# Layer 1 of a four-layer kernel: score products read from PSUM on VectorE, sums over heads by identity products on TensorE, expert shares applied to an input

## The chip, the cores and the metric

The kernel runs on one core of one Trainium2 chip. A core has a matrix engine (TensorE, PE; its weight loads are listed as PEld), a vector engine (VectorE, DVE), an activation engine (ScalarE, ACT), a general engine (GpSimd, POOL) and queues for transfers. They run side by side and wait for each other by semaphores; each works through its own queue in order. SBUF is the working memory, PSUM the memory that TensorE writes its products to. The metric is the time of one execution in microseconds (us), the median of several runs. A profile is one execution recorded by the hardware; L12 is line 12 of the kernel before.

## The reference

Four layers, each `x = x + s * g` with `s` an attention-like branch and `g` the silu of a feed-forward branch, both on the layer norm of x. There are 4 sequences of 1024 tokens with 128 features. The change touches only the second layer (called layer 1). Its attention works inside a token, between its 16 heads of 8 features:

```
x = (y_de * mask).reshape(c, t, HEADS, PER_DIM)
q = x @ Wq.T + bq;  k_ = x @ Wk.T + bk;  v = x @ Wv.T + bv
scores = einsum('cthd,ctgd->cthg', q, k_) * scale
attn = entmax15(scores, axis=-1)
out = einsum('cthg,ctgd->cthd', attn, v)
```

The sum over d has 8 terms, the sum over g has 16, and both are different for every token. `entmax15` sorts the 16 scores of a head, takes running sums of the sorted values and of their squares, finds a threshold from them, and squares what lies above it. The feed-forward branch takes two of eight experts for each token:

```
expert_out = einsum('etf,efh->eth', silu(x w1) * (x w3), w2)
out = einsum('te,eth->th', combine, expert_out)
```

`combine` holds a token's weight for each expert, zero for all but two. The kernel computes all eight experts for all tokens and lets `combine` choose.

## The kernel before

Everything is kept in fp32. Layer 1 runs over eight units; a unit is 512 tokens, as four tiles of 128 tokens, tokens on the partitions. For each unit there are two generators, `heads1` for attention and `moe1` for the experts. Each gives work out in steps that end at a `yield`.

`heads1`: for each of the four tiles TensorE multiplies the transposed input with a block-diagonal weight matrix, 384 columns of queries, keys and values (L701); VectorE adds the bias on the way from PSUM to SBUF (L702); POOL multiplies each head's query with each head's key, 2048 products per token (L707); VectorE sums over d with a reduction (L710). Then VectorE sorts the 16 scores of every row in ten min and max steps (`sort16`, L683 and L684; ACT copies the parts that a step leaves alone, L673 and L674). The threshold follows on VectorE, POOL and ACT in turns: z, the distance from the top score (L720, POOL), two running sums (L724 and L725, VectorE), their division by the rank (L730 and L731, POOL), the clamp at zero (L734, VectorE), a square root (L735, ACT), tau (L738, POOL), a comparison with z and a count (L740 and L742, VectorE), the choice of one tau (L743, VectorE, and L744, POOL), and the share of each head (L748, POOL, and L751, VectorE). Last come the values: for each tile POOL multiplies shares and values, 2048 products per token (L756), and VectorE sums over g (L759).

`moe1`: logits (L767), the two best experts (`top2`, L189 to L197), their weights (L773 to L780). Then for each expert two halves of 128 hidden features: two products with 512 token columns (L786 and L788), the silu on ACT (L789), a multiplication on VectorE (L790). The down product puts tokens on the partitions, eight products of 128 columns (L795), and VectorE scales them by the expert's weight and adds them up, four instructions for an expert (L799 and L801). A silu on ACT makes g (L802).

`update` multiplies s by g and adds the result to x, both on POOL (L225 and L226).

`weave` decides the order in which these pieces are written down: it always takes the generator that is least far along, counting each generator's steps against a given number of steps. A unit's attention after its scores, its experts, and the next unit's scores (`upto`) are woven together. The framework then puts the instructions into the engines' queues, by its own scheduling, and the order in a queue can differ from the order in which they were written. Once built, it is fixed. Tiles come from pools: a tag has a number of buffers, and an instruction that writes a new tile waits until the last reader of the buffer's former tile is done. The PSUM pools of layer 1 are "mm" with four buffers, "tr" with two and "o" with two. `transpose_tiles` (L122) transposes by TensorE, and its copies from PSUM go to VectorE (L112) or ACT (L114).

Of the kernel before, what the change touches and what calls it, by code (L numbers as in the profile page):

```python
# [18 lines left out]
P = 128  # L19
# [72 lines left out]
class Kit:  # L92
# [86 lines left out]
    def top2(self, pool, score, n_tiles, tag):  # L179

        nc = self.nc
        shape4 = [P, n_tiles, 8, 8]
        cmp = pool.tile(shape4, F32, tag=tag + "_cmp", name="cmp")
        eq = pool.tile(shape4, F32, tag=tag + "_eq", name="eq")
        rank = pool.tile([P, n_tiles, 8], F32, tag=tag + "_rank", name="rank")
        before = self.c("before").rearrange("p (e j) -> p e j", j=8)
        other = score.unsqueeze(2).to_broadcast(shape4)
        own = score.unsqueeze(3).to_broadcast(shape4)
        nc.vector.tensor_tensor(cmp, other, own, ALU.is_gt)  # L189
        nc.vector.tensor_tensor(eq, other, own, ALU.is_equal)  # L190
        flat = lambda a: a.rearrange("p t e j -> p t (e j)")
        wide = self.c("before").unsqueeze(1).to_broadcast([P, n_tiles, 64])
        nc.gpsimd.tensor_tensor(flat(eq), flat(eq), wide, ALU.mult)
        nc.gpsimd.tensor_tensor(flat(cmp), flat(cmp), flat(eq), ALU.add)
        nc.vector.tensor_reduce(rank, cmp, AX.X, ALU.add)
        two = pool.tile([P, n_tiles, 8], F32, tag=tag + "_two", name="two")
        nc.vector.tensor_scalar(two, rank, 2.0, None, op0=ALU.is_lt)  # L197
        return two
# [417 lines left out]
def layer1(k, W, x_all, eps5, ps):  # L616

    nc, tc = k.nc, k.tc
    with tc.tile_pool(name="l1", bufs=1) as p1, tc.tile_pool(name="l1d", bufs=2) as p2:
# [6 lines left out]
        def start(half, b):  # L626
# [13 lines left out]
            s, g = (p2.tile([P, HT, D], F32, tag=tag, name=tag) for tag in ("s", "g"))  # L640
            return x, s, g, heads1(k, W, p1, p2, ps, xnT, maskedT, s, keep), moe1(k, W, p1, p2, ps, xnT, g)
# [8 lines left out]
        for n in range(len(units)):  # L650
            x, s, g, heads, moe = now
            parts = [(heads, 19), (moe, 18)]
            if n + 1 < len(units):
                now = start(*units[n + 1])
                parts.append((upto(now[3]), 4))
            weave(*parts)
            k.update(x, s, g)
# [34 lines left out]
def heads1(k, W, p1, p2, ps, xnT, maskedT, s, keep):  # L692
# [3 lines left out]
    qkv = p2.tile([P, 4, 3, P], F32, tag="qkv", name="qkv")  # L696
    score = p2.tile([P, 4, 16, 16], F32, tag="score", name="score")
    for t in range(4):
        lhsT = maskedT if maskedT is not None and t == 0 else xnT[:, t * P : (t + 1) * P]
        pq = ps.tile([P, 512], F32, tag="mm", name="pq")  # L700
        nc.tensor.matmul(pq[:, 0:384], lhsT, W["bd"].rearrange("p n c -> p (n c)"), start=True, stop=True)  # L701
        nc.vector.tensor_tensor(  # L702
            qkv[:, t].rearrange("p n c -> p (n c)"), pq[:, 0:384], W["bias"].rearrange("p n h d -> p (n h d)"), ALU.add
        )
        heads = lambda n: qkv[:, t, n, :].rearrange("p (h d) -> p h d", d=8)
        prod = p2.tile([P, 16, 16, 8], F32, tag="prod", name="prod")
        nc.gpsimd.tensor_tensor(  # L707
            prod, heads(0).unsqueeze(2).to_broadcast([P, 16, 16, 8]), heads(1).unsqueeze(1).to_broadcast([P, 16, 16, 8]), ALU.mult
        )
        nc.vector.tensor_reduce(score[:, t], prod, AX.X, ALU.add)  # L710
        yield "scores" if t == 3 else None
# [4 lines left out]
    new = lambda name: p2.tile([P, R * 16], F32, tag=name, name=name)  # L716
# [34 lines left out]
    nc.vector.scalar_tensor_tensor(attn, t1, 0.0, t1, op0=ALU.max, op1=ALU.mult)  # L751
    for t in range(4):
        a = attn.rearrange("p (t h g) -> p t h g", t=4, g=16)[:, t]
        v = qkv[:, t, 2, :].rearrange("p (g d) -> p d g", d=8)
        prod = p2.tile([P, 16, 8, 16], F32, tag="prod", name="prod")
        nc.gpsimd.tensor_tensor(  # L756
            prod, a.unsqueeze(2).to_broadcast([P, 16, 8, 16]), v.unsqueeze(1).to_broadcast([P, 16, 8, 16]), ALU.mult
        )
        nc.vector.tensor_reduce(s[:, t, :].rearrange("p (h d) -> p h d", d=8), prod, AX.X, ALU.add)  # L759
        yield  # L760


def moe1(k, W, p1, p2, ps, xnT, g):
# [5 lines left out]
    nc.vector.tensor_copy(logit.rearrange("p t e -> p (t e)"), pl[:, 0:32])  # L769
    two = k.top2(p2, logit, HT, "m1")  # L770
# [9 lines left out]
    nc.vector.tensor_tensor(comb, comb, best.unsqueeze(2).to_broadcast([P, HT, 8]), ALU.mult)  # L780
    for e in range(8):
        yield
        h = p2.tile([P, 2, 512], F32, tag="h", name="h")
        for c in range(2):
# [3 lines left out]
            nc.tensor.matmul(pu, W["w3"][:, e, c * P : (c + 1) * P], xnT, start=True, stop=True)  # L788
            nc.scalar.activation(h[:, c, :], pg, AF.Silu)  # L789
            nc.vector.tensor_tensor(h[:, c, :], h[:, c, :], pu, ALU.mult)  # L790
        yield
        po = ps.tile([P, 4, D], F32, tag="o", name="po")
        for t in range(4):
            for c in range(2):
                nc.tensor.matmul(po[:, t, :], h[:, c, t * P : (t + 1) * P], W["w2"][:, e, c, :], start=(c == 0), stop=(c == 1))  # L795
        for t in range(4):
            w = comb[:, t, e : e + 1]
            if e == 0:
                nc.vector.tensor_scalar(g[:, t, :], po[:, t, :], w, None, op0=ALU.mult)  # L799
            else:  # L800
                nc.vector.scalar_tensor_tensor(g[:, t, :], po[:, t, :], w, g[:, t, :], op0=ALU.mult, op1=ALU.add)  # L801
    nc.scalar.activation(g, g, AF.Silu)  # L802
# [1131 lines left out]
def tile_kernel(ctx: ExitStack, tc: tile.TileContext, I, out):  # L1934
# [30 lines left out]
    with tc.tile_pool(name="w2", bufs=1) as w2:  # L1965
        with tc.tile_pool(name="raw2", bufs=1) as raw2:
            W2 = load2(k, w2, raw2, I)
            with ExitStack() as st:
                ps = PsumTags(st, tc, {"mm": 4, "tr": 2, "o": 2}, "ps1")
# [36 lines left out]
```

## Time and profile before

Three runs took 3631.48, 3636.46 and 3638.12 us; the median is 3636.46. The profiled execution took 3631.55 us, its span is 3629.8 us.

| what | value |
|---|---|
| profiled execution; its span | 3631.55; 3629.8 us |
| busy over the span: PE, VectorE, ACT, POOL | 64%, 69%, 41%, 37% |
| layer 1, from the first query product to the last addition to x | 579.6 to 1391.4 us |
| busy in 578 to 1395 us: PE, VectorE, ACT, POOL | 457.7, 640.2, 212.3, 469.8 us |
| granted TensorE clock there | 0.77 of full speed |
| transfers there | 3 GB/s |

In the lists of groups a row gives line, engine, operation, output<-inputs, shapes, number of instructions, then busy time and mean length, then the idle time of the engine just before these instructions and what ended it. An fp32 product is listed as two TensorE instructions. [...] In timelines the columns are the start, the time covered, engine, line, operation, tiles and the number of instructions put together in the row.

### The profile page before, as it was taken

The numbers are of one execution on the slowest core, as the hardware profiler recorded it, in microseconds if no ns is written. First come the engines' busy times: TensorE is split into PE (matmuls) and PEld (weight loads), VectorE is DVE, ScalarE is ACT, GpSimd is POOL, SyncE is SP. The second block draws the span as 40 slices with busy tenths as digits, with TensorE's granted clock in tenths as the row PEclk, the third lists the DMA queues.
The fourth block names the chain that finished last, engine by engine and source line by source line (L and its number), as shares of the span: only waits on it lengthen the run. The fifth ranks groups of instructions, "written<-read, shape, count | busy, mean of one in ns | idle before, by whom it ended". The sixth has DMA issues, their size and how long they took to land. (4 is left out here: it accounts for less than half of the span.)

```text
span 3629.8 us, 51798 instructions
## 1 busy us (share of the span) xinstructions
PE 2314.1 (64%) x18736; PEld 1376.0 (38%) x18737; DVE 2504.9 (69%) x5864; ACT 1470.2 (41%) x3148; POOL 1347.2 (37%) x1089
## 2 busy tenths in 40 slices
PE   4877875555655564966643400058888889889885
PEld 2555553333333332642100100035555555545553
DVE  5555557778888775556778677744787677677767
ACT  4555543222222224244432300015665655565553
POOL 3344444665555653225365222243122122212222
PEclk9888987778877786966555555566776766767666
DMA  3000001000000001211334399727466466566553
GB/s 82 1 1 1 1 1 31 0 0 1 0 1 0 0 0 44 96 58 34 69 52 73 63 111 102 117 70 211 127 196 199 139 191 200 156 181 199 170 167 108
DMA packets 486565, 295.16 MB, mean 81 GB/s; under 512 B 165392, under 2 KB 473484, under 8 KB 485284
## 3 DMA queue, kind: packets, MB, share of 16 engines
q1 hardware_dynamic: 485156, 287.65, 32.9%
q10 hardware_dynamic: 1152, 4.19, 0.4%
q8 instruction: 147, 2.41, 0.3%
q14 instruction: 110, 0.90, 0.1%
HBM read 156.43 MB, written 134.74 MB: 80 GB/s over the span
## 5 line engine op out<-in xcount | busy, mean ns | idle before, releaser
L1808 POOL TENSOR_SCALAR_AFFINE_SELECT rel<-rel 128x512 f32<-128x512 f32 x288 | 179.9, 635 | 765.3 <-DMA rel<-flat 493.1
L1863 ACT ACTIVATE neg<-neg,low 128x640 f32<-128x640 f32 (+7 forms) x512 | 390.5, 766 | 165.5 <-DVE low L1856 164.8
L1649 DVE STREAM_TRANSPOSE wT<-neg 128x640 f32<-128x640 f32 (+7 forms) x512 | 364.3, 756 | 54.0 <-ACT neg L1863 29.6
L1841 PE MATMUL score<-k,q 8*128 8x512 f32 (+3 forms) x1536 | 331.2, 742 | 90.0 <-DVE low L1856 89.6
L1856 DVE CUSTOM_DVE_ANT_0 neg<-score,rel,low 128x128 f32<-128x128 f32 (+3 forms) x448 | 218.1, 519 | 149.7 <-PE score L1841 71.7
L795 PE MATMUL po<-w,h 128*128 128x128 f32 x1024 | 172.3, 329 | 170.6 <-DVE h L790 170.5
L1777 PE MATMUL pr<-emb,q 8*128 8x256 f32 x1024 | 257.7, 566 | 30.4 <-ACT r L1779 22.8
L1877 PEld LDWEIGHTS po<-wT,vb 128*32 128x32 f32 x10240 | 200.2, 136 | 150.4 <-issue 101.2
L1877 PE MATMUL po<-wT,vb 128*32 128x64 f32 (+1 forms) x10240 | 234.6, 253 | 31.3 <-issue 17.5
L795 PEld LDWEIGHTS po<-w,h 128*128 128x128 f32 x1024 | 161.4, 238 | 235.9 <-DVE h L790 208.1
L1779 ACT COPY r<-pr 128x512 f32<-128x512 f32 x256 | 138.9, 582 | 160.7 <-PE pr L1777 77.0
L1777 PEld LDWEIGHTS pr<-emb,q 8*128 8x128 f32 x1024 | 152.9, 265 | 127.7 <-ACT r L1779 61.6
L1841 PEld LDWEIGHTS score<-k,q 8*128 8x128 f32 x1536 | 123.4, 251 | 165.6 <-DVE low L1856 103.2
L707 POOL TENSOR_TENSOR prod<-qkv 128x2048 f32<-128x2048 f32 x32 | 153.2, 4789 | 75.7 <-DVE qkv L702 74.2
L786 PE MATMUL pg<-xnT,w 128*128 128x512 f32 x256 | 145.2, 651 | 56.1 <-DVE qkv L702 53.5
L756 POOL TENSOR_TENSOR prod<-rest,qkv 128x2048 f32<-128x2048 f32 x32 | 171.6, 5385 | 12.0 <-DVE rest L751 10.7
L1856 DVE CUSTOM_DVE_ANT_0 neg<-score,rel 128x512 f32<-128x512 f32 (+3 forms) x320 | 149.6, 521 | 34.8 <-PE score L1841 30.9
L122 PE MATMUL pt<-const_sb,o 128*128 128x128 f32 x8 | 3.0, 432 | 266.1 <-DVE o L1376 266.1
L788 PE MATMUL pu<-xnT,w 128*128 128x512 f32 x256 | 138.7, 625 | 11.0 <-ACT h L789 5.7
L789 ACT ACTIVATE h<-pg 128x512 f32<-128x512 f32 x128 | 75.5, 596 | 167.7 <-PE pg L786 167.2
L987 ACT ACTIVATE h<-ph 128x512 bf16<-128x512 f32 (+1 forms) x128 | 72.0, 590 | 173.7 <-PE ph L986 171.3
L986 PE MATMUL ph<-xin,upT 128*128 128x512 bf16 (+1 forms) x128 | 74.0, 612 | 103.1 <-DVE xin L980 103.1
(613 smaller groups left out, 5875.9 us busy)
## 6 DMA issues: line engine op xcount, KB each, us to landing
flat<-r SPq DMA_DIRECT2D x256, 256.0 KB, 2.8
rel<-flat SPq DMA_DIRECT2D x112, 512.0 KB, 3.9
flat<-r SPq DMA_DIRECT2D x256, 128.0 KB, 2.9
rel<-flat SPq DMA_DIRECT2D x96, 256.0 KB, 4.2
kt<-kd SPq DMA_DIRECT2D x64, 128.0 KB, 7.2
qt<-qd SPq DMA_DIRECT2D x64, 128.0 KB, 6.7
ktc<-ktd SPq DMA_DIRECT2D x32, 256.0 KB, 5.7
kdc<-kdd SPq DMA_DIRECT2D x32, 256.0 KB, 6.0
```

The costliest lines, as they stand in the source:

```text
L707: nc.gpsimd.tensor_tensor(prod, heads(0).unsqueeze(2).to_broadcast([P, 16, 16, 8]), heads(1).unsqueeze(1).to_broadcast([P, 16, 16, 8]), AL ...
L756: nc.gpsimd.tensor_tensor(prod, a.unsqueeze(2).to_broadcast([P, 16, 8, 16]), v.unsqueeze(1).to_broadcast([P, 16, 8, 16]), ALU.mult)
L786: nc.tensor.matmul(pg, W["w1"][:, e, c * P : (c + 1) * P], xnT, start=True, stop=True)
L795: nc.tensor.matmul(po[:, t, :], h[:, c, t * P : (t + 1) * P], W["w2"][:, e, c, :], start=(c == 0), stop=(c == 1))
L1649: nc.vector.transpose(weights[at, pair][j][:, t % 2, 0 : (t + 1) * P], S[j][:, 0 : (t + 1) * P])
L1777: nc.tensor.matmul(to[:, m, :], q[at, t * P : (t + 1) * P], W["emb"][at, i, :], start=True, stop=True)
L1779: nc.scalar.copy(r[:, n], to)
L1808: nc.gpsimd.affine_select(out=rel[:, :, slot(back), :], in_=rel[:, :, slot(0), :], compare_op=op, fill=fill, base=0, pattern=[[0, 4], [-si ...
L1841: nc.tensor.matmul(sc[:, j, 0 : last - first], q[at(j), 1 + t * P : 1 + n], kk[at(j), first:last], start=True, stop=True)
L1856: nc.vector.tensor_tensor_reduce(out=neg[:, begin:last], in0=sc[:, j, begin - first : last - first], in1=rel[:, j, slot : slot + (last - b ...
L1863: nc.scalar.activation(neg[:, 0:n], neg[:, 0:n], AF.Exp, bias=here, scale=-1.0, accum_out=group["sums"][:, j, t : t + 1])
L1877: nc.tensor.matmul(o[32 * j : 32 * j + 32, 2 * pair + m.start : 2 * pair + 2, :], vb[:, kb, j].rearrange("p a d -> p (a d)"), weights[j][: ...
```

## The change

Attention. The bias is now added by TensorE itself, as a second product of a row of ones with one row of the bias into the same PSUM tile. ACT copies keys and values to SBUF; the queries stay in PSUM. VectorE, not POOL, multiplies queries, read in PSUM, with keys, read in SBUF, and writes the products with d outermost. TensorE sums over d: eight products of the identity matrix with 256 columns each, added up in one PSUM tile, which ACT copies to the scores. The products of a tile are summed one step later than they are made. The share of each head is made by two ACT instructions, Relu and Square, in place of one on VectorE. POOL still multiplies shares and values, now with g outermost, and TensorE sums over g with sixteen identity products of 128 columns for each tile; ACT copies the four sums to s.

Experts. The weights of a unit are split into three bf16 parts (`thirds`), transposed, and for each expert spread over all partitions by a product with a constant (`shares`). VectorE multiplies the transposed input with that share, and this weighted input goes into the linear branch (w3), so that the weight is already in the hidden features. The down product now has w2 as its stationary side and 512 token columns, and adds up all eight experts in one PSUM tile. The result is transposed (gT), so `update` turns it back by TensorE, multiplies s by it on VectorE and adds to x on POOL. `top2` reads one of its two inputs in PSUM.

The tags "tr" and "o" have one buffer, and "sc" and "v" are new with one each. Tiles z, zz and cum have one buffer instead of two. The step counts of `weave` are changed.

```
--- before.py
+++ after.py
-        other = score.unsqueeze(2).to_broadcast(shape4)
+        other = (score if again is None else again).unsqueeze(2).to_broadcast(shape4)
...
+        def update(x, s, gT):
+
+            k.transpose_tiles(
+                ps, "tr", [gT[:, t * P : (t + 1) * P] for t in range(HT)], s.rearrange("p t d -> p (t d)"),
+                lambda out, in_: nc.vector.tensor_tensor(out, out, in_, ALU.mult),
+            )
+            nc.gpsimd.tensor_tensor(x, x, s, ALU.add)
...
-            parts = [(heads, 19), (moe, 18)]
+            parts = [(heads, 20), (moe, 11)]
             if n + 1 < len(units):
                 now = start(*units[n + 1])
-                parts.append((upto(now[3]), 4))
+                parts.append((upto(now[3]), 5))
             weave(*parts)
-            k.update(x, s, g)
+            update(x, s, gT)
...
+    def add_up(t, prod):
+        psc = ps.tile([P, 256], F32, tag="sc", name="psc")
+        for d in range(8):
+            nc.tensor.matmul(psc, k.ident, prod[:, d].rearrange("p h g -> p (h g)"), start=(d == 0), stop=(d == 7))
+        nc.scalar.copy(score[:, t].rearrange("p h g -> p (h g)"), psc)
...
-        nc.tensor.matmul(pq[:, 0:384], lhsT, W["bd"].rearrange("p n c -> p (n c)"), start=True, stop=True)
+        nc.tensor.matmul(pq[:, 0:384], lhsT, W["bd"].rearrange("p n c -> p (n c)"), start=True, stop=False)
+        nc.tensor.matmul(pq[:, 0:384], k.c("ones")[0:1, :], W["bias"][0:1].rearrange("p n h d -> p (n h d)"), start=False, stop=True)
+        nc.scalar.copy(kv[:, t].rearrange("p n c -> p (n c)"), pq[:, P : 3 * P])
+
+        each = [P, 8, 16, 16]
+        prod = p2.tile(each, F32, tag="prods", name="prod")
         nc.vector.tensor_tensor(
-            qkv[:, t].rearrange("p n c -> p (n c)"), pq[:, 0:384], W["bias"].rearrange("p n h d -> p (n h d)"), ALU.add
+            prod, pq[:, 0:P].rearrange("p (h d) -> p d h", d=8).unsqueeze(3).to_broadcast(each),
+            kv[:, t, 0, :].rearrange("p (g d) -> p d g", d=8).unsqueeze(2).to_broadcast(each), ALU.mult,
         )
...
-        nc.vector.tensor_reduce(score[:, t], prod, AX.X, ALU.add)
-        yield "scores" if t == 3 else None
+        if t:
+            add_up(t - 1, before)
+        before = prod
+        yield
+    add_up(3, before)
+    yield "scores"
...
-    nc.vector.scalar_tensor_tensor(attn, t1, 0.0, t1, op0=ALU.max, op1=ALU.mult)
+    nc.scalar.activation(attn, t1, AF.Relu)
+    nc.scalar.activation(attn, attn, AF.Square)
+    yield
+    pv = ps.tile([P, 4, P], F32, tag="v", name="pv")
...
+    def values(t, prod):
+        for g in range(16):
+            nc.tensor.matmul(pv[:, t, :], k.ident, prod[:, g].rearrange("p h d -> p (h d)"), start=(g == 0), stop=(g == 15))
...
-        prod = p2.tile([P, 16, 8, 16], F32, tag="prod", name="prod")
+        each = [P, 16, 16, 8]
+        prod = p2.tile(each, F32, tag="prodv", name="prod")
         nc.gpsimd.tensor_tensor(
-            prod, a.unsqueeze(2).to_broadcast([P, 16, 8, 16]), v.unsqueeze(1).to_broadcast([P, 16, 8, 16]), ALU.mult
+            prod, attn.rearrange("p (t h g) -> p t g h", t=4, g=16)[:, t].unsqueeze(3).to_broadcast(each),
+            kv[:, t, 1, :].rearrange("p (g d) -> p g d", d=8).unsqueeze(2).to_broadcast(each), ALU.mult,
         )
-        nc.vector.tensor_reduce(s[:, t, :].rearrange("p (h d) -> p h d", d=8), prod, AX.X, ALU.add)
...
+    values(3, before)
+    nc.scalar.copy(s.rearrange("p t d -> p (t d)"), pv.rearrange("p t d -> p (t d)"))
...
+    thirds = k.thirds(p2, ps, comb, "m1")
+    yield
+    po = ps.tile([P, 512], F32, tag="o", name="po")
+    share = k.shares(ps, thirds, 0)
...
+    def down(e, h):
+        for c in range(2):
+            nc.tensor.matmul(po, W["w2"][:, e, c, :], h[:, c, :], start=(e == 0 and c == 0), stop=(e == 7 and c == 1))
...
+        xin = p2.tile([P, 512], F32, tag="xin", name="xin")
+        nc.vector.tensor_tensor(xin, xnT, share, ALU.mult)
+        share = k.shares(ps, thirds, e + 1) if e < 7 else None
...
-            nc.tensor.matmul(pu, W["w3"][:, e, c * P : (c + 1) * P], xnT, start=True, stop=True)
+            nc.tensor.matmul(pu, W["w3"][:, e, c * P : (c + 1) * P], xin, start=True, stop=True)
...
-        for t in range(4):
-            w = comb[:, t, e : e + 1]
-            if e == 0:
-                nc.vector.tensor_scalar(g[:, t, :], po[:, t, :], w, None, op0=ALU.mult)
-            else:
-                nc.vector.scalar_tensor_tensor(g[:, t, :], po[:, t, :], w, g[:, t, :], op0=ALU.mult, op1=ALU.add)
-    nc.scalar.activation(g, g, AF.Silu)
+        if before is not None:
+            down(e - 1, before)
+        before = h
+        yield
+    down(7, before)
+    nc.scalar.activation(gT, po, AF.Silu)
...
-                ps = PsumTags(st, tc, {"mm": 4, "tr": 2, "o": 2}, "ps1")
+                ps = PsumTags(st, tc, {"mm": 4, "tr": 1, "o": 1, "sc": 1, "v": 1}, "ps1")
```

`thirds` and `shares` were there before, for the third layer (L200 to L221).

## The prediction

> **What bounds the kernel now.** I read three views: the table of stretches, the costliest groups of layer 1, and the timelines of single engines through one unit. Stretches first, at 100 us per row (time, busy us with instructions per engine, granted clock):
>
> ```profile
> 780.00:880.00 100.00, 52.05 (x208) 31.61 (x207) 79.92 (x112) 24.66 (x43) 58.65 (x20) 0.78 0.00 0
> 880.00:980.00 100.00, 55.43 (x213) 32.58 (x212) 82.26 (x103) 22.77 (x38) 57.13 (x20) 0.78 0.00 0
> ```
>
> VectorE is busy 80%, PE 55% at a clock of 0.78. A unit takes 101.2 us: the adds into x_all (L226) start at 707.27 and, six units later, at 1314.69. Layer 1 ends with the last add, 1391.4. The groups of layer 1 (busy us, mean ns | idle before):
>
> ```profile
> L795 PE MATMUL po<-w,h 128*128 128x128 f32 x1024 | 172.3, 329 | 170.6 <-DVE h L790 170.5
> L756 POOL TENSOR_TENSOR prod<-rest,qkv 128x2048 f32<-128x2048 f32 x32 | 171.6, 5385 | 12.0 <-DVE rest L751 10.7 <-DVE s L759 1.3
> L707 POOL TENSOR_TENSOR prod<-qkv 128x2048 f32<-128x2048 f32 x32 | 153.2, 4789 | 75.7 <-DVE qkv L702 74.2 <-DVE ln_rs L138 1.5
> L790 DVE TENSOR_TENSOR h<-h,pu 128x512 f32<-128x512 f32 x128 | 85.0, 676 | 0.0
> L759 DVE TENSOR_REDUCE s<-prod 128x128 f32<-128x2048 f32 x32 | 73.1, 2283 | 86.5 <-POOL prod L756 86.5
> L710 DVE TENSOR_REDUCE score<-prod 128x256 f32<-128x2048 f32 x32 | 72.8, 2274 | 22.6 <-POOL prod L707 22.6
> L720 POOL TENSOR_TENSOR z<-sorted,top 128x1024 f32<-128x1024 f32 x8 | 15.5, 1934 | 94.1 <-DVE sorted L684 70.6 <-ACT h L789 23.5
> ```
>
> A unit ends with four value products on POOL, each followed by a reduction that VectorE waits for: 86.5/8 = 10.8 us idle. The VectorE timeline shows a second loss, a sort step that lasts seven times its own length:
>
> ```profile
> 911.28 0.68 DVE L683 TENSOR_TENSOR sorted<-sorted 128x512 f32<-128x512 f32 x1
> 911.88 4.95 DVE L684 TENSOR_TENSOR sorted<-sorted 128x512 f32<-128x512 f32 x1
> 945.91 5.71 DVE L724 TENSOR_TENSOR_SCAN cum<-keep,z 128x1024 f32<-128x1024 f32 x1
> 953.71 2.27 DVE L725 TENSOR_TENSOR_SCAN rest<-keep,zz 128x1024 f32<-128x1024 f32 x1
> ```
>
> POOL ran L707 at 911.28 to 916.28 and 944.96 to 949.46. The PE timeline gives the price of fp32:
>
> ```profile
> 911.05 2.07 PE L786 MATMUL pg<-xnT,w 128*128 128x512 f32 x2 [27.57 <-DVE qkv L702]
> 926.55 1.72 PE L795 MATMUL po<-w,h 128*128 128x128 f32 x14
> 929.19 1.02 PE L786 MATMUL pg<-xnT,w 128*128 128x512 f32 x2
> 930.05 1.02 PE L788 MATMUL pu<-xnT,w 128*128 128x512 f32 x2
> ```
>
> Each fp32 product is two passes. From start to start a warm 512-column product takes 930.05 - 929.19 = 0.86 us, a 128-column pass 1.72/14 = 0.123. After idling it is twice that.
>
> [...] the reduction over 2048 takes 2.27. [...] L756 steps over 8 elements and takes 5.38, L707 does not and takes 4.79, L720 with an inner broadcast 1.93 for half the size.
>
> **The change part by part**, per unit.
> VectorE loses L702 (4 x 0.55), L710 and L759 (8 x 2.28), L801/L799 (32 x 0.34), L751 1.2: 32.5 us, and the lock waits on L707. It gains four score products (2.25 each: 9.0, bounds 2.2 and, if the strided PSUM read costs double, 4.5), eight weighings of xin (5.4), the split into thirds (1.5), the update (0.7): 16.6. ACT gains some 8 us of copies and two activations, which hide behind PE except Relu and Square (2 x 1.06, inside piece 2's start).
> POOL loses L707 (19) and one update multiply (1.6). Its value product now has inner steps 0 and 1: bounds 3.9 (twice L720) and 5.4 (L756); I take 4.2.
> PE gains most. Score sums: 4 x 8 products of 256 columns, at 0.43 each 13.7. Value sums: 4 x 16 of 128 columns, 128 passes x 0.123 = 15.7. Bias: 4 x 0.64. Shares in bf16, one pass: 8 x 0.215 = 1.7. L795 (15.7) becomes 16 products of 512, 13.7. PE warm before: 27.4 + 15.7 + 2.6 + 2 = 48; after: 27.4 + 13.7 + 13.7 + 15.7 + 5.1 + 1.7 + 2 = 79.
>
> No DMA is added or moved. Layer 1's PSUM tags "tr" and "o" keep one buffer instead of two; transposes, logits and expert sums come in that order on PE anyway, so I cost that at nothing (a few tenths if a copy is late).
>
> So neither engine is full; the queues' order decides. The built order of the changed kernel puts on VectorE, per unit: entmax chain of this unit, thirds, experts 0 to 6 with the next unit's score products between, then that unit's sort and scans up to the clamp (L734), then this unit's update. On PE the last score sum of the next unit stands behind expert 6. So the sort waits for PE (behind it on VectorE stand scans, clamp and update, and POOL's z waits for them), and the experts wait for thirds, which stand behind the clamp. The cycle is a sum:
>
> 1. Clamp to the first expert product. L734 ended at 962.87 and L740 began at 966.49: 3.6. Then, new: POOL's update add ahead of the rank products, which VectorE's compare and rank reduction wait for, 1.4 + 1.5; compare 1.2, small ones 0.5, count 1.2, first score product 2.3, equality 1.3, POOL multiply 2.5 (L744), reduction with small ones 2.4, PE transposes, copy, share 1.4. Sum 19.3.
> 2. PE from there to the last score sum: experts 0 to 6, 28 products x 0.855 = 23.9; six pairs of down products 10.3; shares 1.7; three query products with bias 3.8; three score sums 10.3: 50.0. Two stalls: the first Silu waits in ACT's queue behind Relu, Square and a table load (0.8), and the four "mm" buffers make expert 1 wait for the second score product (1.4). Sum 52.2[...].
> 3. Last sum, ACT copy, sort: 0.7.
> 4. Sort to clamp. Sort steps start to start 10.5, ACT copies between 1.2, two h products of expert 7 1.2. POOL's third value product needs a buffer that the first value sum frees, and that sum stands right behind the last score sum: it falls into the sort and locks it, 4.0. top and z 2.4; the fourth value product follows z, as L707 did, and locks the scan 4.2; scans 4.5; two POOL multiplies 4.8; add and clamp 1.9. Sum 34.7.
>
> Cycle: 106.9 us against 101.2.
>
> Whole layer. Today the sort of unit 0 starts at 612.1. Now the four score sums and query products (18.8 on PE from 580, half cold) let it start at 603. Unit 0's experts run beside its own sort: 60 us to unit 1's sort (PE 53, VectorE 58 by its queue). Clamp of unit 1: 603 + 60 + 34.7 = 698. Six cycles: 641, so 1339. The last unit has no score product to make: 17.0 to its first expert, 42.8 for eight experts, 15.7 for the value sums, 0.8 of transposes, 2.9 for copy, multiply and add: 1418. That is 27 us later than 1391.4. The transposes for layer 2 (L122, 1367 to 1369.7) no longer hide in POOL's tail: 2 us. The profiled execution took 3631.55 with a span of 3629.8; 29 more is 3660.6. The median of the runs shown is 4.9 above that execution, their lowest 0.07 below; I add half: 3663.
>
> What is costed at nothing: score products 2 to 4 (6.8 of VectorE), xin and h (15 us) are covered by PE's 52; first and second value products by the same. Were that cover gone, VectorE's 22 us would come into the cycle in part.
>
> **Rivals.**
> *No collisions* (one mechanism, faster). [...] 8.2 us leave piece 4: cycle 98.7, and six of them give 3663 - 49 = 3614. For: my times on POOL hang on an estimated 4.2. Against: buffer and queue order force both places, and L724 shows the second in the kernel before. It decides below 102.3 us a cycle, when the two locks cost 3.6 together.
> *Busy time rules* (much faster): units overlap until PE's 79 us, plus a few cold ones, are the limit, say 84: 3663 - 6 x 23 = 3525. For: VectorE is the busiest engine today and loses 16 us net with locks on top. Against: the order in the queues.
> *Strided PSUM reads cost double* (slower): the first score product and the buffer stall each grow 2.25: 6 x 4.5 = 27 more, 3690. For: no row of before reads so. [...]
> *A break-even*: pieces 1 and 4 each 2 us shorter than walked, 3639, no change that can be told.
>
> **How the numbers follow.** My forecast has 0.57 (own range 3644 to 3690: four us a cycle either way), strided reads 0.09, no collisions 0.17, busy time 0.08, break-even 0.09. Slower by over 0.2% (7 us, about what a measurement can tell from no change): 0.66; same 0.09; faster 0.25. The range leaves out the busy-time case and the far end of strided reads: 3604 to 3702.
>
> **What would show it.** Right: adds into x_all 105 to 109 us apart; PE without gaps for some 50 us at clock near 1, then mostly idle or cold; sort steps and the first scan lasting 4 to 5 us beside the new value products; VectorE busy near 60%, its longest waits for PE's score sum and for thirds. Wrong: adds under 101 us apart; value products of 3.9 us that end before the sort; 256-column passes unlike 0.215 us; score products away from 2.25; experts starting well before 17 us after the clamp.

## The result, and the profile after

The changed kernel takes 3717.07 us (median; 3707.84 to 3723.96) against 3635.82 for the kernel before (3631.48 to 3638.12): a ratio of 1.0227, interval 1.0205 to 1.0248, so slower by some 81 us. The profiled execution took 3713.24 us with a span of 3711.5, 81.7 more than before. The forecast was 3663, slower by 27: the sign was right, but the loss is three times the forecast one, and the time lies above the range, whose upper end was 3702.

Nearly all of it lies in layer 1. Its last addition to x ends at 1468.0 us instead of 1391.4 (76.6 us), and what follows takes 2243.5 us instead of 2238.4 (5). The additions are 112.2 us apart on average, 101.2 before, 106.9 forecast. Lines below are numbered by the changed kernel: L723 is the score product, L711 the score sum, L786 POOL's value product, L780 the value sum, L717 and L718 query product and bias, L834 and L836 an expert's two products, L755 the clamp, L692 and L693 the sort.

The same table of stretches as before (time, busy us with instructions for PE, weight loads, VectorE, ACT, POOL, then granted clock):

```profile
780.00:880.00 100.00, 80.34 (x295) 49.45 (x294) 60.11 (x75) 28.72 (x52) 32.54 (x14) 0.83 0.00 0
880.00:980.00 100.00, 80.13 (x301) 47.90 (x300) 62.41 (x75) 27.62 (x51) 33.72 (x14) 0.85 0.00 0
```

VectorE fell from about 80% to 61%, POOL from 58% to 33%, and PE rose from 52 and 55% to 80%. None of them is full. The groups of layer 1 (busy us, mean ns of one | idle before them and who ended it):

```profile
L711 PE MATMUL psc<-prod,const_sb 128*128 128x256 f32 x512 | 134.3, 419 | 32.6 <-DVE prod L723 32.1 <-ACT score L712 0.4
L786 POOL TENSOR_TENSOR prod<-rest,kv 128x2048 f32<-128x2048 f32 x32 | 132.9, 4163 | 381.1 <-PE pv L780 361.7 <-ACT rest L773 19.4
L723 DVE TENSOR_TENSOR prod<-pq,kv 128x2048 f32<-128x2048 f32 x32 | 123.1, 3850 | 39.4 <-ACT kv L719 36.9 <-PE psc L711 2.5
L838 DVE TENSOR_TENSOR h<-h,pu 128x512 f32<-128x512 f32 x128 | 87.5, 686 | 125.2 <-PE pu L836 107.8 <-ACT h L837 17.1 <-issue 0.3
```

VectorE and POOL now wait for PE (107.8 and 361.7 us), where in the kernel before PE waited for VectorE. A score product lasts 3.85 us; the forecast priced it at 2.25. POOL's value product was estimated at 4.2 and takes 4.16 on average. The value product of the kernel before, with a step of eight elements, took 5.38, which is 29% more; no run separates that step from the other differences between the two.

VectorE's timeline, sort and scans of one unit (start, us, and in brackets the idle time before):

```profile
908.04 0.69 DVE L692 TENSOR_TENSOR sorted<-score 128x512 f32<-128x512 f32 x1 [4.82 <-ACT score L712]
...
911.24 4.51 DVE L693 TENSOR_TENSOR sorted<-sorted 128x256 f32<-128x256 f32 x1
...
920.55 4.36 DVE L692 TENSOR_TENSOR sorted<-sorted 128x512 f32<-128x512 f32 x1
...
931.10 2.29 DVE L745 TENSOR_TENSOR_SCAN cum<-keep,z 128x1024 f32<-128x1024 f32 x1 [2.11 <-POOL z L741]
```

There are two locks of some four us, as forecast. A lock is here what the timelines show: POOL ran L786 from 911.09 to 915.25 and from 919.82 to 924.36, and the two sort steps that began meanwhile ended at 915.75 and 924.91, after 4.51 and 4.36 us; in the same sort the other steps on 256 columns take 0.42 to 0.64 us and those on 512 columns 0.68 to 0.70. In this unit the fourth value product came ahead of z and locked a second sort step, and the scan took 2.29 us; in the five units of eight where it follows z, the scan takes 6.12 us. It comes to the same: sort to clamp differs by less than half a microsecond between the two.

PE's timeline in another unit shows what the forecast did not have (L220 is the share):

```profile
1074.32 1.02 PE L836 MATMUL pu<-xin,w 128*128 128x512 f32 x2
1078.51 0.79 PE L780 MATMUL pv<-prod,const_sb 128*128 128x128 f32 x2 [3.17 <-POOL prod L786]
1079.10 1.49 PE L717 MATMUL pq<-bdw,xnT 128*128 128x384 f32 x2
1080.51 1.64 PE L718 MATMUL pq<-bias,const_sb 1*128 1x384 f32 x2
1081.95 0.63 PE L220 MATMUL pb<-thirds,pick 24*128 24x512 bf16 x1
1082.51 2.08 PE L834 MATMUL pg<-xnT,w 128*128 128x512 f32 x2
1084.38 1.92 PE L836 MATMUL pu<-xin,w 128*128 128x512 f32 x2
```

A single product of the first value sum of the unit at hand stands behind expert 0 in PE's queue. It waits 3.17 us for POOL, and the first three of the following 512-column products take 1.9 to 2.1 us instead of 1.02 (the third starts at 1086.09 and takes 1.91). The granted clock was 1.00 from 1071 to 1076 us, 0.54 from 1078.5 to 1088.7 and 1.00 again from there to 1098; products in a stretch of such a low clock are called cold here, those at a clock of 1.00 warm.

### The profile page after: what moved, and what is told of

It reads as the page before. It is cut to its first block, busy times and chain, and to the rows that moved or that the text cites. A ratio compares the mean times of both kernels' runs of the same rounds, so it can differ in the third digit from the quotient of the medians.

```text
span 3711.5 us, 53600 instructions
## 1 busy us (share of the span) xinstructions
PE 2601.5 (70%) x19696; PEld 1538.1 (41%) x19697; DVE 2403.2 (65%) x5644; ACT 1503.5 (41%) x3236; POOL 1145.9 (31%) x1049
## 5 line engine op out<-in xcount | busy, mean ns | idle before, releaser
L1819 PE MATMUL pr<-emb,q 8*128 8x256 f32 x1024 | 258.4, 570 | 29.7 <-ACT r L1821 22.1
L786 POOL TENSOR_TENSOR prod<-rest,kv 128x2048 f32<-128x2048 f32 x32 | 132.9, 4163 | 381.1 <-PE pv L780 361.7
L838 DVE TENSOR_TENSOR h<-h,pu 128x512 f32<-128x512 f32 x128 | 87.5, 686 | 125.2 <-PE pu L836 107.8
L711 PE MATMUL psc<-prod,const_sb 128*128 128x256 f32 x512 | 134.3, 419 | 32.6 <-DVE prod L723 32.1
L780 PE MATMUL pv<-prod,const_sb 128*128 128x128 f32 x1024 | 130.7, 291 | 34.7 <-POOL prod L786 34.7
L723 DVE TENSOR_TENSOR prod<-pq,kv 128x2048 f32<-128x2048 f32 x32 | 123.1, 3850 | 39.4 <-ACT kv L719 36.9
L780 PEld LDWEIGHTS pv<-prod,const_sb 128*128 128x128 f32 x1024 | 129.2, 207 | 46.6 <-POOL prod L786 41.6
L834 PE MATMUL pg<-xnT,w 128*128 128x512 f32 x256 | 145.6, 652 | 3.1 <-DVE prod L723 3.1
```

Of the source, the lines that this page charges most:

```text
L711: nc.tensor.matmul(psc, k.ident, prod[:, d].rearrange("p h g -> p (h g)"), start=(d == 0), stop=(d == 7))
L780: nc.tensor.matmul(pv[:, t, :], k.ident, prod[:, g].rearrange("p h d -> p (h d)"), start=(g == 0), stop=(g == 15))
L786: nc.gpsimd.tensor_tensor(prod, attn.rearrange("p (t h g) -> p t g h", t=4, g=16)[:, t].unsqueeze(3).to_broadcast(each), kv[:, t, 1, :].re ...
L834: nc.tensor.matmul(pg, W["w1"][:, e, c * P : (c + 1) * P], xnT, start=True, stop=True)
L1819: nc.tensor.matmul(to[:, m, :], q[at, t * P : (t + 1) * P], W["emb"][at, i, :], start=True, stop=True)
```

## The experiments

Each cycle can be cut as the forecast cut it: end of the clamp to the first expert product (part 1), from there to the first sort step (parts 2 and 3), sort to the end of the clamp (part 4). The table has the means in us over the six cycles from the second clamp on, read from the timelines, with the median times. Each ratio is to runs of the kernel before made alongside that kernel, whose medians went from 3635.8 to 3639.6, so a ratio can differ a little from the quotient of the times:

| kernel | part 1 | parts 2, 3 | part 4 | cycle | time, us | ratio to before |
|---|---|---|---|---|---|---|
| forecast | 19.3 | 52.9 | 34.7 | 106.9 | 3663 | |
| changed kernel | 20.3 | 57.9 | 34.0 | 112.2 | 3717.1 | 1.0227 |
| half_scores | 20.7 | 51.4 | 34.1 | 106.2 | 3680.7 | 1.0110 |
| unit_step | 19.1 | 57.4 | 34.0 | 110.5 | 3716.2 | 1.0211 |
| unit2 | 19.2 | 56.8 | 34.0 | 110.0 | 3688.8 | 1.0136 |
| keys_only | 19.2 | 56.8 | 34.0 | 110.1 | 3697.5 | 1.0166 |
| three_bufs | 20.9 | 59.4 | 30.3 | 110.6 | 3699.9 | 1.0170 |
| late3 | 19.5 | 54.3 | 34.3 | 108.2 | 3689.6 | 1.0152 |
| unit_late3 | 18.0 | 54.3 | 34.3 | 106.6 | 3672.7 | 1.0107 |

The kernels below have no such sum of parts, since their experts and their sort overlap otherwise:

| kernel | additions to x apart, us | time, us | ratio to before, interval |
|---|---|---|---|
| before | 101.2 | 3635.8 | |
| attn_only | 98.9 | 3623.6 | 0.9964, 0.9948 to 0.9980 |
| experts_only | 98.7 | 3620.6 | 0.9949, 0.9934 to 0.9963 |
| eo_early | 96.0 | 3605.3 | 0.9915, 0.9896 to 0.9934 |
| w12 | 99.0 | 3644.2 | 1.0011, 1.0003 to 1.0019 |
| early_w14 | 104.9 | 3663.0 | 1.0061, 1.0042 to 1.0080 |
| early | 93.6 | 3579.0 | 0.9838, 0.9813 to 0.9862 |
| early_u | 93.3 | 3568.5 | 0.9806, 0.9787 to 0.9825 |

### Which half of the change costs: attn_only and experts_only

attn_only takes `moe1` and `update` from the kernel before; the core of it:

```
-            x, s, gT, heads, moe = now
-            parts = [(heads, 20), (moe, 11)]
+            x, s, g, heads, moe = now
+            parts = [(heads, 20), (moe, 18)]
...
-            update(x, s, gT)
+            k.update(x, s, g)
...
-    thirds = k.thirds(p2, ps, comb, "m1")
...
-        nc.vector.tensor_tensor(xin, xnT, share, ALU.mult)
...
-            nc.tensor.matmul(pu, W["w3"][:, e, c * P : (c + 1) * P], xin, start=True, stop=True)
+            nc.tensor.matmul(pu, W["w3"][:, e, c * P : (c + 1) * P], xnT, start=True, stop=True)
```

> The attention of the changed kernel with the experts of the kernel before: no thirds, no shares, no weighted input, down products with tokens on the partitions. Theory A (the experts' wait for the router's weights, which stand on VectorE behind the clamp, is what makes the cycle a sum of a TensorE part and a chain): here the experts' first products need only the transposed input, TensorE works during the chain, and the cycle falls by 10 us or more below 112, so the time is below 3640. Theory B (the identity sums, 29 us of TensorE a unit, are what costs): the time stays above 3690. In between neither holds alone.

experts_only takes `heads1` and the PSUM tags from the kernel before, and steps (19, 11, 4) in the weave.

> The attention of the kernel before (products on POOL, sums by reductions on VectorE) with the experts of the changed kernel. Theory A (the wait for the weights costs with any attention): slower than the kernel before, 3640 to 3680, with experts that start some 15 us or more after the unit's start. Theory B (the identity sums are the cost and the experts' edit is a gain, since VectorE loses 32 scalings of 0.34 us and gains 8 products of 0.68): faster than the kernel before, 3590 to 3625.

Each half alone is a little faster than the kernel before, by 13 and 16 us against the 3636.6 measured alongside, and both intervals lie below 1. Together they are slower by 81. For attn_only theory A held (3623.6, below 3640). PE's timeline of attn_only fits: a clamp ended at 916.2, and the first expert product starts 3.9 us later, where the changed kernel needs 20.

```profile
916.95 1.62 PE L709 MATMUL pq<-bdw,xnT 128*128 128x384 f32 x2 [5.34 <-DVE logit L796]
918.50 1.64 PE L710 MATMUL pq<-bias,const_sb 1*128 1x384 f32 x2
920.07 2.08 PE L813 MATMUL pg<-xnT,w 128*128 128x512 f32 x2
```

For experts_only theory A failed, and the time lies in the range of B (3590 to 3625). The wait for the weights is there (PE idle for 22.65 us), but it does not make the kernel slower: the sort had begun at 903.84, beside that wait, and stands behind no sum of PE.

```profile
923.52 0.60 PE L212 MATMUL pt<-ident,three 128*24 128x128 bf16 x4 [22.65 <-DVE three L209]
924.75 1.01 PE L220 MATMUL pb<-thirds,pick 24*128 24x512 bf16 x2 [0.64 <-DVE thirds L112]
925.69 2.07 PE L808 MATMUL pg<-xnT,w 128*128 128x512 f32 x2
```

So neither edit is the loss by itself, and the reading that follows is tested next. Experts behind the thirds is one wait, sort behind PE's last score sum is the other; with both, PE's part and the threshold chain follow one another in a ring.

### Opening the ring by order alone: early, w12, early_w14

early:

```
-            while next(heads) != "scores":
+            for _ in range(2):
+                next(moe)          # logits, best two; weights, thirds
+                yield
+            while next(heads) != "scores":
...
-            parts = [(heads, 20), (moe, 11)]
+            parts = [(heads, 20), (moe, 9)]
...
-                parts.append((upto(now[3]), 5))
+                parts.append((upto(now[3], now[4]), 7))
...
-    pl = ps.tile([P, 512], F32, tag="o", name="pl")
+    pl = ps.tile([P, 512], F32, tag="tr", name="pl")
```

> Order alone: the next unit's router (logits, best two, thirds) is written down one unit earlier, with that unit's scores, and its logits use the PSUM tag tr; the work is that of the changed kernel. Theory A (each half of the change opens one wait, experts behind the thirds and sort behind TensorE's last score sum, and only both together close a ring in which TensorE's part and the threshold chain follow one another): with the first wait gone, TensorE works during the sort, the cycle falls from 112 to 92 to 100, the time to 3590 to 3640. Theory B (the work itself is too much: identity sums of 29 us a unit, cold clock, locks): 3690 or more.

w12 changes one number, `upto(now[3]), 5` to `12`. early_w14 is early with 14 in place of 7.

> Order alone: the step count of the next unit's scores in the weave is 12 instead of 5, so its score products and sums come before or beside the first experts and the sort runs beside the later experts; the thirds stay where they are. Theory A: with the second wait gone the ring is open too; a unit then takes thirds 12 us, eight experts with sums some 65, values and update some 18, 95 us in all, the time 3590 to 3640. Theory B: 3690 or more.

> Both orders at once: the next unit's router a unit earlier and its scores at 14 steps instead of 7. Theory A: both waits are gone, what is left is TensorE's own work (79 us a unit when warm, by the forecast) plus the last values and the update of each unit, 86 to 95 us a cycle, 3540 to 3600. Theory B: 3690 or more. A third case: if it is not faster than the two single orders, TensorE's queue (value sums that wait for POOL at the end of each unit) is the next bound.

early runs the same arithmetic as the changed kernel and takes 3579.0 us, 138 less than it and 57 less than the kernel before: faster than theory A's own range, whose lower end was 3590. Its logits also use another PSUM tag, and that move alone was not run. One cycle each as a stretch, first of the changed kernel:

```profile
1055.10:1168.00 112.90, 90.72 (x329) 53.19 (x329) 67.28 (x75) 28.94 (x53) 31.47 (x15) 0.85 0.00 1
```

and of early:

```profile
1079.70:1171.50 91.80, 84.26 (x332) 50.09 (x333) 61.72 (x79) 29.10 (x51) 32.26 (x14) 0.96 0.00 1
```

PE does the same products in both. In early it is busy 84 of 92 us at a clock of 0.96: TensorE is now nearly full, and its busy time is what the forecast's rival "busy time rules" had put at 84 us a cycle.

w12 opens the other wait. Here is the start of a sort on VectorE, and what PE had just begun:

```profile
972.48 1.13 PE L834 MATMUL pg<-xnT,w 128*128 128x512 f32 x2
973.19 0.69 DVE L692 TENSOR_TENSOR sorted<-score 128x512 f32<-128x512 f32 x1
```

These are the first products of expert 2, so five more experts run on PE beside the sort and the chain after it; in the changed kernel the sort stands behind expert 6. w12 gains 73 us, to 3644.2, just over theory A's range and level with the kernel before. early_w14 opens both and is slower than either (3663.0): theory A's 3540 to 3600 was missed, and the third case, not faster than the two single orders, came in. In early_w14 POOL's z comes late, the value products with it, and at the end of a unit PE has nothing ahead of the value sums:

```profile
1128.58 6.55 PE L783 MATMUL pv<-prod,const_sb 128*128 128x128 f32 x32 [3.31 <-POOL prod L789]
1137.98 5.33 PE L783 MATMUL pv<-prod,const_sb 128*128 128x128 f32 x32 [2.85 <-POOL prod L789]
```

A value sum that takes 3.73 us in the changed kernel at 924.80, where PE did not wait for it, takes 5.3 to 6.6 here. Whether this is all of early_w14's 11 us a cycle over early was not tested, so the cause of that loss stays open.

early_u is early with the order of queries and keys of unit2, below.

> The earlier router (early) together with keys and queries in the other order (unit2). With the ring open TensorE is busy 85 of 93 us a cycle and VectorE 62, so theory A expects the shorter score products to be worth little now: 3560 to 3580 against 3579 for early. If the first score product were still on a path through VectorE, it would give the 2 us a cycle again that it gave in unit2, and 3550 to 3562.

It takes 3568.5 us, in theory A's range. Of the 28 us by the medians that the shorter score product gives in unit2 (15 by the spans of the profiled executions), 10 (6 by the spans) are left once TensorE is nearly full.

eo_early puts the same earlier router on experts_only (steps 19, 9 and 6).

> The attention of the kernel before, the experts of the changed kernel, and the router a unit earlier. In experts_only a unit took 98.7 us although TensorE was busy only 59 of it and VectorE 70. Theory A (the ring needs both halves; here the sort never stood behind TensorE, so that an earlier router opens nothing): a gain of less than 3 us a cycle, 3600 to 3621. A rival (the wait for the weights alone cost as much as in the whole change): 3540 to 3580.

The time, 3605.3, is in theory A's range, and so is the gain of 2.7 us a cycle. The same step gave 18.6 us a cycle in the whole change.

### Is PE's own work on the path: half_scores

```
-        for d in range(8):
-            nc.tensor.matmul(psc, k.ident, prod[:, d].rearrange("p h g -> p (h g)"), start=(d == 0), stop=(d == 7))
+        for d in range(4):
+            nc.tensor.matmul(psc, k.ident, prod[:, d].rearrange("p h g -> p (h g)"), start=(d == 0), stop=(d == 3))
```

> Left out: four of the eight identity products of every score sum, so half of the sum over d. Theory A (VectorE's sort stands behind TensorE's last score sum, and the experts ahead of that sum fill TensorE without a gap, so that TensorE's own work is on the path): a sum falls from 3.65 to 1.85 us, three of them lie between the first expert and the sort, the cycle falls by 5 to 6 us, and with the first unit (four sums) the time by some 40 to 45, to 3670 to 3680. Theory B (VectorE's or POOL's chain sets the pace and TensorE's sums are beside it): the time falls by less than 10 us, to above 3707.

Parts 2 and 3 fell from 57.9 to 51.4 us, the time by 36, just short of the 40 to 45 that theory A gave. Theory A holds: the three sums between the first expert and the sort are 5.4 us shorter by its figures, and the parts fell by 6.5. What PE does there is paid in full.

### The score product: unit_step, unit2, keys_only

```
-            prod, pq[:, 0:P].rearrange("p (h d) -> p d h", d=8).unsqueeze(3).to_broadcast(each),
-            kv[:, t, 0, :].rearrange("p (g d) -> p d g", d=8).unsqueeze(2).to_broadcast(each), ALU.mult,
+            prod, pq[:, 0:P].rearrange("p (d h) -> p d h", d=8).unsqueeze(3).to_broadcast(each),
+            kv[:, t, 0, :].rearrange("p (d g) -> p d g", d=8).unsqueeze(2).to_broadcast(each), ALU.mult,
```

with the columns of the query and key weights and biases put in the same order once, in `prepare1`.

> The columns of queries and keys are put in another order (d outermost), so that the score product reads the query in PSUM and the key in SBUF without a step of eight elements; the rest is the changed kernel. Theory A (the steps of eight make the score product 3.85 us long, and one product per unit, the first, stands on the path that sets the end, with a second one in part by way of the four buffers of the tag mm): the product falls to 2.2 to 2.4 us, the cycle from 112.2 to 109 to 110.5, the time from 3717 to 3692 to 3706. Theory B (the length comes from the query being repeated along the innermost axis, or from PSUM itself): it stays at 3.8 and so does the time. Theory C (the score products are covered by TensorE's experts): the product falls to 2.3, the time by less than 5 us.

> As unit_step, but the bias row is put in order by one product into PSUM at the start of layer 1: in unit_step the copies of the bias sat in ACT's queue at the very start of the program, waited 13.7 and 12.4 us for transfers there, and pushed the first layer's last addition from 571.6 to 585.8, while layer 1 itself took 882.3 us instead of 895.2 up to its last addition. Theory A (one long score product per unit is on the path): without that stall 3699 to 3708, layer 1 some 10 to 16 us shorter than in the changed kernel. Theory C (the products are covered): 3712 to 3720.

> Only the keys are put with d outermost, the queries stay as they are: the score product then reads keys in SBUF one after another, and the query in PSUM still with steps of eight between heads. If the step of the key in SBUF makes the product long, it takes 2.3 us here, and the time is that of unit2, 3680 to 3700. If it is the read from PSUM, it stays at 3.85 and the time at 3710 to 3725. A length in between means both.

unit_step took 3716.2 us, which missed theory A's 3692 to 3706 and reads like "covered"; but its cycle fell to 110.5 us, and its own set-up stalled the start by 14 us (the first layer's last addition starts at 585.8 instead of 571.6). unit2 without that stall takes 3688.8, 28 us under the changed kernel and below even theory A's range; in the profiled execution the last addition starts at 1449.3 instead of 1466.8, 17.5 us earlier. keys_only tells which operand it is. The score product's group in keys_only, and below it the same in the kernel with both in order, unit2:

```profile
L732 DVE TENSOR_TENSOR prod<-pq,kv 128x2048 f32<-128x2048 f32 x32 | 73.1, 2286 | 42.4 <-ACT kv L728 39.5 <-PE psc L720 2.9
L733 DVE TENSOR_TENSOR prod<-pq,kv 128x2048 f32<-128x2048 f32 x32 | 73.1, 2286 | 41.7 <-ACT kv L729 39.2 <-PE psc L721 2.5
```

It takes 2.29 us with only the keys in order, while the query is still read in PSUM with its steps between heads, and putting the query in order as well changes nothing. The time, 3697.5, is in the range for that case, too. So the query's step in PSUM costs nothing here, and the key's step of eight elements in SBUF costs 1.56 us per product. No run reads the query from SBUF, so reading in PSUM was not compared with reading in SBUF; but at 2.29 us the product is as short as the reductions over 2048 elements in the kernel before (2.27 and 2.28).

### The locks: three_bufs

```
-        prod = p2.tile(each, F32, tag="prodv", name="prod")
+        prod = pv4.tile(each, F32, tag="prodv", name="prod")     # a pool with three buffers
```

> Three buffers instead of two for POOL's value products (s and gT give up their second buffers for it). The forecast put two locks of VectorE by POOL into every cycle, the third value product in the sort (4.0 us) and the fourth beside the first scan (4.2). Theory L (they cost what they last): the third product now runs before the sort, the fourth takes its place in the sort, and nothing stands beside the scan; sort to clamp falls from 34 to 30 us, the cycle by 4, the time to 3686 to 3697. Theory M (a lock displaced is no lock removed, or VectorE has slack there): less than 8 us, 3709 or more.

VectorE's timeline of three_bufs has one long sort step left where there were two:

```profile
1016.86 4.51 DVE L693 TENSOR_TENSOR sorted<-sorted 128x256 f32<-128x256 f32 x1
...
1026.19 0.69 DVE L692 TENSOR_TENSOR sorted<-sorted 128x512 f32<-128x512 f32 x1
...
1033.10 2.29 DVE L745 TENSOR_TENSOR_SCAN cum<-keep,z 128x1024 f32<-128x1024 f32 x1 [2.11 <-POOL z L741]
```

Part 4 fell by 3.7 us, as theory L says. But parts 1 to 3 grew by 2.1: the built order now puts a value product ahead of expert 1 in three of the six cycles instead of two. The time, 3699.9, lies between the two theories, which this extra wait explains.

### The order in PE's queue: late3 and unit_late3

```
+        if t == 1:
+            yield
+            yield
+            yield
         if t:
             values(t - 1, before)
...
-            parts = [(heads, 20), (moe, 11)]
+            parts = [(heads, 23), (moe, 11)]
```

> Order alone: three more steps of the attention generator before the first value sum is written down (23 steps instead of 20). In the changed kernel one product of the first value sum stands in TensorE's queue behind expert 0 in two units of six, waits 3.0 and 3.2 us for POOL there and leaves TensorE cold for the next ones; in two other units the first score sum is split around expert 0. Here all units have one order, with the first value sum behind expert 7. Theory H (these orders make the part from clamp to sort 78.2 us on average instead of the 74.4 to 75.4 of the two units without them): clamp to sort falls to 74 to 76 in every unit, the cycle by 2.5 to 4, the time to 3693 to 3703, unless value sums that come later lengthen sort to clamp. Theory K (TensorE's wait there is covered): no change, 3712 or more.

> late3 with queries and keys in the other order (unit2): the two terms that the forecast left out, the long score product and TensorE's wait for a value product, both taken away. If they add up, 28 and 20 us leave the 3717 of the changed kernel, 3665 to 3677, which is near the forecast of 3663; what is left over it would be TensorE's prices (an expert 5.66 us instead of 5.35, a query with bias 1.57 instead of 1.28, a score sum 3.65 instead of 3.41). If they overlap on one path: 3680 to 3690.

In the changed kernel the two cycles with a value product behind expert 0 have 60.0 and 61.4 us in parts 2 and 3, the two with a split score sum 57.5 and 57.4 (and 22.1 and 20.5 in part 1), and the two with neither 56.0 and 54.9. In late3 all six have 54.1 to 54.9. The time fell by 27 us, to just under the 3693 to 3703 of theory H, which holds. Its stretch from first expert to sort, in the cycle whose clamp ended at 1039.5:

```profile
1058.90:1113.20 54.30, 53.54 (x149) 26.59 (x149) 26.04 (x25) 13.88 (x23) 8.49 (x3) 1.00 0.00 1
```

PE is busy 53.5 of 54.3 us at full clock: nothing but its own work is left there. unit_late3 takes 3672.7 us, within the 3665 to 3677 of the case that the two terms add up. The cycles nearly add up: 4.0 and 2.2 us less alone, 5.6 together. The medians do so less well: 27 and 28 us alone, 44 together. By the spans of the profiled executions it is 21 and 15 alone and 41 together, so single comparisons of medians carry some us that the cycles do not explain.

## Why the forecast had the right sign and the wrong size

**The cycle as a sum: right.** The experts' wait for the thirds and the sort's wait for the last score sum were named as what decides. Opening either wait gives back 73 to 138 us with no work removed (w12, early), and halving PE's score sums gives back what they last (half_scores). That each edit alone is a gain was not forecast: the step-by-step walk of the whole change does not show it.

**Part 2, PE from the first expert to the last score sum: the step that failed most.** The forecast walked one order of PE's queue and took it for all units. The built order is not the same in each: a value product behind expert 0 in two of six cycles, a score sum split around expert 0 in two others. These orders cost 4.0 us a cycle on average (112.2 against 108.2 in late3), 3.6 of them in parts 2 and 3. The walk priced every product of this part warm (0.855 us from start to start for 512 columns); after the wait of 3.17 us for POOL three of them took 1.9 to 2.1 us instead of 1.02.

**Score product 2.25 us: failed.** It took 3.85, 1.6 more, and only one of the four shows on the path: part 1 is 19.5 in late3 and 18.0 in unit_late3, while parts 2 and 3 are 54.3 in both. So the stall of 1.4 us that the forecast gave to the second score product, by way of the "mm" buffers, does not depend on it. The forecast's 2.25 was the author's estimate: the nearest rows of the kernel before are the reductions over 2048 elements (2.27 and 2.28 us), and no row there read as the new product does. Its rival "strided PSUM reads cost double" had a step as the reason, but at the wrong operand: the product takes 3.85 us with the key stepping over eight elements in SBUF, and 2.29 with the keys in order and the query still stepping in PSUM (keys_only). Where between one and eight elements the loss begins, no run shows.

**What is left over.** With both terms removed the cycle is 106.6 against 106.9 forecast. That agreement is in part luck, since two smaller errors cancel in it. Part 1 is 18.0 (forecast 19.3). Parts 2 and 3 are 54.3 (52.9): a query with its bias takes 1.57 us instead of 1.28, a score sum 3.65 instead of 3.43, a share 0.32 instead of 0.215 and a warm expert 5.66 from one start to the next instead of 5.35, so that PE's work up to the last sum is 52.9 us instead of 50.0, while the stalls are 0.8 us instead of 2.2 (late3, 1058.96 to 1112.61, with 0.76 us of idle).

**Sort to clamp, 34.7: right** (34.0), with its locks. **No collisions: rejected** as a description of the changed kernel; removing one lock gave 3.7 of the 8.2 us. **Busy time rules: rejected** for the built order, near the truth for early. **A break-even: rejected**: of its two pieces one was 1.0 us longer than walked (part 1) and one 0.7 shorter (part 4).

**The start: too early, the other step that failed.** Unit 0's sort was forecast at 603 and began at 615.2, and unit 1's sort followed 65.0 us later instead of 60. The forecast gave the four score sums and query products 18.8 us on PE, "half cold". They took 32.0, from 582.4 to 614.4: all eight query and bias products ran cold before the first sum (1.63 to 1.65 us each, at a granted clock of 0.50, where the next two took 0.81 and 0.91), 12.6 us with them, and the first sum took 5.4 us instead of 3.65 warm. In unit_late3 the sort began at 612.8 and the next followed 62.9 later. These two, 12.7 us, are more than the 10 us between its 3672.7 and the forecast.

**The sum.** Against the forecast's span of 3658.8, the measured 3711.5 is 52.7 more: start 12.2, first to second sort 5.0, six cycles 31.8 (673.2 against 641.4 from 106.9 each), tail 1.6, after the layer 3.0, and 0.9 less in unit 1's sort to clamp.

## What to carry to other kernels

A change that moves work between engines can be a gain in each half and a loss as a whole: look for two waits that close a ring, and open one by order before judging the work. Read the built order of every unit in each queue, not of one; in the changed kernel a single product that waited 3.17 us for another engine had three products of 1.9 to 2.1 us instead of 1.02 behind it. When a VectorE instruction is priced, look at the innermost step of each operand, in SBUF too: a step of eight elements there made 3.85 us of 2.29.

## What the runs showed of the hardware that was not expected

- A VectorE product of 2048 fp32 results took 3.85 us with one SBUF operand stepping over eight elements and 2.29 us with that operand in order. Putting the other operand in order as well, which is read in PSUM and repeated 16 times, made no difference.
- Order alone (in the fastest with one PSUM tag exchanged) moved one set of instructions between 3579 and 3717 us. The best version that was run, early_u, is 67 us below the kernel before.
